# First Toeplitz blocks of a separable convolution: from the taps in SBUF instead of by way of DRAM

## The chip, the cores and the metric

The kernel runs on one core of a Trainium2 chip. The core has five engines with instruction queues of their own: PE (TensorE, matrix products), DVE (VectorE), ACT (ScalarE), POOL (GpSimd) and SP (SyncE, which here only issues transfers). Sixteen DMA engines move data between DRAM and the on-chip memory SBUF, whose 128 partitions are the rows of every tile. PE writes its results to PSUM. The metric is the device time of one execution in microseconds (us); lower is better. Everything is float32.

## The reference

The input x has 4 images of 64 channels of 256 x 256. Two layers are computed.

The first is a long convolution per channel. Its filter is the outer product of two 1-D filters of 256 taps for each channel, an "X" and a "Y" filter. Each comes from a small network with sine activations over a positional embedding, times an exponential decay:

```python
h = jnp.sin(freq * (z @ w1 + b1))
h = jnp.sin(freq * (h @ w2 + b2))
h = jnp.sin(freq * (h @ w3 + b3))
h = h @ wo
decay = jnp.exp(-t * jnp.abs(deltas))
return h * decay
...
k = jnp.einsum('ijk,imk->ijmk', hx, hy)[0]
...
y = jnp.fft.irfft2(u_f * k_f, s=(fft_size, fft_size))[..., :L, :L]
out = y + x * bias[:, None, None]
```

The FFTs are twice as long as the image, so this is a causal 2-D convolution, and since the filter is an outer product it splits into two 1-D passes. The second layer whitens the channels: a mean and a 64 x 64 covariance over every ninth pixel, five Newton-Schulz steps towards its inverse square root, and a product of that matrix with the centred pixels.

## The kernel before

**Taps.** The two filter networks run side by side as one 128-row problem (rows 0 to 63 the X filters, 64 to 127 the Y filters), at L154 to L176. Each layer is a matrix product, an argument reduction on DVE and a sine on ACT. The last step, L176, multiplies by the decay on DVE and writes `taps`, a part of the SBUF tile `scratch`: 128 rows of 256 taps, followed by 128 zeros. Row f * 64 + c holds the taps of filter f (0 or 1) of channel c, reversed in time.

**Toeplitz blocks.** A 1-D causal convolution by matrix products needs, for each filter and channel, the taps shifted by one from row to row. `load_toeplitz` (L188) makes them while loading: row p of a block is the row of taps read from element p on. A block tile `toep` holds, for a round of 8 channels (`CG`), 128 rows, 2 filters, 8 channels and 256 columns. It is loaded in halves of 64 rows (`half`); where the filter number and the half differ, the first 64 columns aren't needed and are skipped. The transfers read the taps from DRAM. For that the taps are stored at L177 (SP) and L178 (ACT) into a small array `g0_d`, which holds the 16 rows of the first round, and at L179 (POOL) into `g_d`, which holds all 128 rows and is read by the later rounds.

**The first round's loads.** L562 lists seven pairs of loads in order, as (filter, first channel, last channel): (0, 0, 2), (0, 2, 4), (0, 4, 6), (1, 0, 2), (0, 6, 8), (1, 2, 4), (1, 4, 8). The lower half of each pair is issued on SP, the upper on ACT. They wait for the stores into `g0_d`. Behind them SP issues the loads of the second image (L566) and, later, those of further images.

**Filler products.** `busy(n)` (L149) gives PE n products of an idle tile. PE takes its instructions in program order, so `busy(22)` at L181 stands between the last product of the filter networks and the first one of the convolution. Each float32 product is two instructions.

**Convolution.** The work goes over `steps`, pairs of a round g of 8 channels and an image n, and in each over channel pairs. The first pass (filter 0) is followed by a copy out of PSUM that swaps the halves (tile `o1`), the second pass (filter 1) by a multiply-add with the bias back into the x tile. In the steady state `group` (L394) does the first pass of one channel pair and the second pass of an earlier one together, in `toeplitz_products` (L203, products at L220). The first two channel pairs have no partner, so `half_group` (L266) does their first pass alone, in `toeplitz_alone` (products at L252, tile `ph`; copies at L286 on ACT and DVE). Its first products read both halves of the blocks of filter 0 of channels 0 and 1. The results go to the DRAM arrays `y_d`, and the ninth pixels are packed for the covariance.

**Whitening and output.** After the last convolution, the covariance (L333) and the Newton-Schulz steps follow, and then the output stage: tiles `yi` are loaded back from `y_d`, multiplied by the whitening matrix (L635), shifted (L639 ACT, L640 DVE) and stored to `out`.

**Order.** From L557 on everything stands under `manual_schedule`: every engine's instructions keep the order in which the program writes them. Each engine takes its own queue in order, and an instruction that waits holds what is behind it on that engine. Semaphores for the data dependences are put in by the framework.

Of the kernel before, what the change touches and what calls it, by code (L numbers as in the profile page):

```python
# [45 lines left out]
NB, C, L = 4, 64, 256  # L46
P, H2 = 128, 2
EMB, ORDER = 33, 64
PIX = L * L
CG = 8  # L50
HP = P // 2
# [13 lines left out]
def conv_whiten_kernel(ctx: ExitStack, tc: tile.TileContext, a: dict, out: bass.AP):  # L65
    nc = tc.nc
# [12 lines left out]
    g_d = dram.tile([P, GW], F32, tag="g", name="g_d")  # L79
# [17 lines left out]
    mask = const.tile([P, NB, H2, STEP], I32, tag="mask", name="mask")  # L97
    bias = const.tile([P, C], F32, tag="bias", name="bias")

    def load_x(t, g, n, c):  # L100
        nc.sync.dma_start(
            out=t[:, c : c + 2],
            in_=x[n, g][:, c : c + 2],
        )
# [16 lines left out]
    for n in range(NB):  # L121
        t = spool.tile([P, FP], F32, tag="samp", name=f"samp{n}")
# [7 lines left out]
    rows = const.tile([P, STEP], F32, tag="rows", name="rows")  # L130
# [8 lines left out]
    taps = scratch[:, 11:13, :].rearrange("p a w -> p (a w)")[:, 0:GW]  # L139
# [9 lines left out]
    def busy(times):  # L149
        p = psA.tile([P, P], F32, tag="psA", name="busy")  # L150
        for _ in range(times):
            nc.tensor.matmul(p, lhsT=idle[:, 0:P], rhs=idle[:, P : 2 * P], start=True, stop=True)  # L152

    hs, wt = [zw[:, u * P : (u + 1) * P] for u in range(2)], zw[:, L : L + P]  # L154
    for i in range(3):
        for u in range(2):
            pm = psA.tile([P, P], F32, tag="psA", name=f"pm{i}_{u}")
            nc.tensor.matmul(pm, lhsT=wt, rhs=hs[u], start=True, stop=True)  # L158
            half = slice(u * P, (u + 1) * P)
# [12 lines left out]
    for u in range(2):  # L172
        half = slice(u * P, (u + 1) * P)
# [2 lines left out]
        nc.vector.tensor_tensor(taps[:, half], pf, decay[:, half], ALU.mult)  # L176
    nc.sync.dma_start(out=g0_d[0:CG], in_=taps[0:CG])  # L177
    nc.scalar.dma_start(out=g0_d[CG:], in_=taps[ORDER : ORDER + CG])  # L178
    nc.gpsimd.dma_start(out=g_d, in_=taps)  # L179
    nc.gpsimd.tensor_copy(rows, mask[:, NB - 1, 0, :])  # L180
    busy(22)  # L181

    def new_toeplitz(g):


        return tpool.tile([P, 2, CG, L], F32, tag="toep", name=f"toep_{g}")

    def load_toeplitz(t, g, f, half, lo=0, hi=CG, issue=nc.sync):  # L188
        source, row = (g0_d, f * CG + lo) if g == 0 else (g_d, f * C + g * CG + lo)


        skip = 0 if f == half else HP
        issue.dma_start(
            out=t[half * HP : (half + 1) * HP, f, lo:hi, skip:],
            in_=bass.AP(
                tensor=source.tensor,
                offset=source.offset + row * GW + skip,
                ap=[[1, HP], [GW, hi - lo], [1, L - skip]],
            ),
        )  # L200


    def toeplitz_products(units, ks):  # L203
# [62 lines left out]
    def half_group(item, which):  # L266

        g, n, c, xt, o1s = item
        jobs = []
        for u in range(2):  # L270
            banks = [
                psA.tile([P, L], F32, tag="psA", name=f"ph{which}_{g}_{n}_{c + u}_{m}")
                for m in range(H2)
            ]
            jobs.append((banks, (o1s[u] if which else xt[:, c + u]), toep[g][:, which, c + u, :]))
        toeplitz_alone(jobs, which)
        if which == 0:
            for u in range(2):
                o1s.append(o1pool.tile([P, H2, L], F32, tag="o1", name=f"o1_{g}_{n}_{c + u}"))
        for m in range(H2):  # L280
            for u in range(2):
                ps = jobs[u][0][m]
                if which == 0:
                    copy = nc.vector.tensor_copy if u else nc.scalar.copy
                    for to, fr in ((slice(0, HP), slice(HP, P)), (slice(HP, P), slice(0, HP))):
                        copy(o1s[u][to, m], ps[fr])  # L286
                else:
                    ch = g * CG + c + u
                    nc.vector.scalar_tensor_tensor(
                        xt[:, c + u, m], xt[:, c + u, m], bias[:, ch : ch + 1], ps,  # L290
                        ALU.mult, ALU.add,
                    )
# [34 lines left out]
    def covariance(n):  # L327

        pc = psA.tile([P, C + 1], F32, tag="psA", name=f"pc{n}")
        for b in range(H2):  # L330
            for j in range(NJ):
                half = slice(C * (j % 2), C * (j % 2 + 1))
                nc.tensor.matmul(  # L333
                    pc[half],
                    lhsT=samp[n][:, b, j, 0:C],
                    rhs=samp[n][:, b, j, :],
                    start=(b == 0 and j < 2),
                    stop=(b == H2 - 1 and j >= NJ - 2),
                    skip_group_check=True,
                )  # L340
        nc.vector.scalar_tensor_tensor(cov, pc, 1.0 / NSAMP, cov, ALU.mult, ALU.add)
# [18 lines left out]
    def load_next():  # L360
        loaded[len(loaded)] = load_y(len(loaded))
# [32 lines left out]
    def group(first, second):  # L394

        units = []
        g1, n1, c1, x1, o1s1 = first
        g2, n2, c2, x2, o1s2 = second
        for u in range(2):
            job2 = (bank(f"p2_{g2}_{n2}_{c2 + u}"), o1s2[u], toep[g2][:, 1, c2 + u, :])  # L400
            job1 = (bank(f"p1_{g1}_{n1}_{c1 + u}"), x1[:, c1 + u], toep[g1][:, 0, c1 + u, :])
            units.append((job1, job2))

        toeplitz_products(units, orders[0])
        orders.reverse()
        for u in range(2):
            o1 = o1pool.tile([P, H2, L], F32, tag="o1", name=f"o1_{g1}_{n1}_{c1 + u}")
            for to, fr in ((slice(0, HP), slice(HP, P)), (slice(HP, P), slice(0, HP))):
                nc.scalar.copy(o1[to], units[u][0][0][fr])  # L409
            o1s1.append(o1)  # L410
            ch = g2 * CG + c2 + u
            nc.vector.scalar_tensor_tensor(  # L412
                x2[:, c2 + u], x2[:, c2 + u], bias[:, ch : ch + 1], units[u][1][0],
                ALU.mult, ALU.add,
            )

        store(second)
        pack(2.92)
# [138 lines left out]
    with tc.manual_schedule(  # L557
        engines={engines.PE, engines.SP, engines.DVE, engines.Activation, engines.Pool}
    ):
        toep = {0: new_toeplitz(0)}  # L560

        for f, lo, hi in ((0, 0, 2), (0, 2, 4), (0, 4, 6), (1, 0, 2), (0, 6, 8), (1, 2, 4), (1, 4, 8)):  # L562
            for half in range(2):
                load_toeplitz(toep[0], 0, f, half, lo, hi, nc.scalar if half else nc.sync)
        for c in range(0, CG, 2):
            load_x(x_tiles[1], *steps[1], c)  # L566
        for i, (g, n) in enumerate(steps):
            xt = x_tiles[i % 4]
            for c in range(0, CG, 2):
                item = (g, n, c, xt, [])  # L570
                if g == C // CG - 1 and n > 0 and c == 2:
                    covariance(n - 1)
                if len(pending) == 2:
                    group(item, pending.pop(0))
                else:
                    half_group(item, 0)
                pending.append(item)
                if i == 0 and c == 6:

                    fold = const.tile([P, C], F32, tag="fold", name="fold")  # L580
                    nc.vector.tensor_tensor(fold, ident[:, 0:C], ident[:, C:P], ALU.add)

                    nc.scalar.activation(bf[:, 0:1], samp[0][:, 0, 0, C : C + 1], AF.Sqrt)
                if i == 1 and c < CG - 2:
                    load_pick(c // 2 * 3, c // 2 * 3 + 3)

                if i + 2 < len(steps):
                    load_x(x_tiles[(i + 2) % 4], *steps[i + 2], c)
                if (i, c) in blocks:
                    tg, part = blocks[i, c]  # L590
                    if part == 0:
                        toep[tg] = new_toeplitz(tg)
                    lo = part % 2 * CG // 2
                    load_toeplitz(toep[tg], tg, part // 4, part // 2 % 2, lo, lo + CG // 2)
                for _ in range(early.get((i, c), 0)):
                    load_next()
        g, n, c, yt, _ = pending[0]
        for item in pending:
            half_group(item, 1)
            pack(1.0)  # L600
            store(item)

        pack()
        i15 = place(2 * C, rows=C).rearrange("p (u c) -> p u c", u=2)
        for u in range(2):
            nc.gpsimd.tensor_scalar(i15[:, u], ident[0:C, 0:C], 1.5, None, ALU.mult)  # L606
        ones = place(P, rows=C)
        nc.gpsimd.memset(ones, 1.0)
        for lo in range(CG // 2, CG, 2):
            pack_by_pe(g, n, yt, slice(lo, lo + 2))  # L610
        spin(4)
        covariance(NB - 1)
        while len(loaded) < len(homes):
            load_next()
        W, shift = whitening(i15, ones)
# [3 lines left out]
    for i, (n, q) in enumerate(pieces):  # L619
# [6 lines left out]
        for w in range(FP // 1024):  # L626
# [15 lines left out]
            if end % part == 0:  # L642

                issue = nc.sync if i == 0 or i + len(homes) >= len(pieces) else nc.gpsimd
# [61 lines left out]
```

## Time and profile before

| what | us |
|---|---|
| median of 3 runs (lowest, highest) | 903.08 (902.95, 903.26) |
| profiled execution: time | 903.93 |
| profiled execution: span from first to last instruction | 902.1 |
| PE busy (share of the span) | 781.2 (87%) |
| DVE busy | 581.5 (64%) |
| ACT busy | 395.5 (44%) |
| L220, the convolution's products: busy for each of the two passes | 579.5 |
| L252, the first round's lone products: start | 16.49 |
| whitening matrix starts from the finished covariance | 632 |

The page's busy figures are shares of the whole span. Up to about 613 us PE works through the convolution; from 670 us on the DMA engines are the busy ones, with 430 GB/s in most slices. The stretch around the change is the first 30 us. Times in the views count from the span's start. A row of the timeline gives the start, the length, the engine, the line, the operation, the tiles (output <- input), how many instructions were merged, and in brackets how long the engine had been idle before and what ended that. "SPq" and "ACTq" are the instruction queues that issue transfers; the length of such a row is the time taken to issue, not to move. A row of the chain of work names the instruction or transfer that the end was waiting for at that time. All three DRAM arrays of taps and blocks go by `g_d` in the profile's tile names.

### The profile page before, as it was taken

What the parts mean: (1) busy time and instruction counts of PE and PEld (TensorE: products, weight loads), DVE (VectorE), ACT (ScalarE), POOL (GpSimd) and SP (SyncE); (2) the same over time, 40 slices, a digit from 0 to 9 for tenths busy, and PEclk for the clock granted to TensorE, in tenths of its full rate; (3) what the DMA queues carried; (4) which work ended last, traced back from release to release, by engine and by line L of the source; (5) the groups of instructions that cost most, each with busy time, mean ns of one, the idle gap of its engine ahead of it and who ended that gap; (6) DMA issues with size and microseconds to landing.
All of it is one profiled execution on the core that took longest, in us unless ns stands there. A gap on an engine that the chain in (4) does not pass through costs nothing.

```text
span 902.1 us, 28046 instructions
## 1 busy us (share of the span) xinstructions
PE 781.2 (87%) x11928; PEld 647.5 (72%) x11928; DVE 581.5 (64%) x801; ACT 395.5 (44%) x676; POOL 14.5 (2%) x40
## 2 busy tenths in 40 slices
PE   8999999999999999999999999999999565666200
PEld 7999999999999999999999999999533111212000
DVE  3487778877888778877888877877688332233200
ACT  2655554545455555545454444442487232233200
POOL 1000000000000000000000000000010000000000
PEclk9999999999999999999999999999999766866755
DMA  7988889798788888888997899979999999999998
GB/s 209 327 262 252 242 261 271 234 273 251 247 263 261 244 264 259 258 250 267 293 275 241 285 351 356 335 237 390 375 401 429 430 432 432 429 434 430 430 430 355
DMA packets 117912, 285.61 MB, mean 317 GB/s; under 512 B 8891, under 2 KB 91116, under 8 KB 110108
## 3 DMA queue, kind: packets, MB, share of 16 engines
q1 hardware_dynamic: 113436, 244.94, 79.0%
q0 software_dynamic: 3056, 37.95, 10.0%
q8 instruction: 95, 1.56, 0.7%
q10 hardware_dynamic: 1296, 0.93, 0.4%
q14 instruction: 29, 0.24, 0.1%
HBM read 149.35 MB, written 134.44 MB: 315 GB/s over the span
## 4 chain that ended last, share of the span: by engine, by line
PE 74%; DMA 11%; another core or an unknown queue 7%; DVE 0%; issue 0%; SPq 0%; ACT 0%; POOLq 0%; DVEq 0%
PE p L220 64%; DMA out_dram<-yi 5%; DMA yi<-y_d 5%; PE po L635 4%; PE pc L333 2%; PE ph L252 1%; PE pk L300 1%; PE spin L442 1%; DMA toep<-g_d 0%; PE busy L152 0%; PE pm L158 0%; SPq L357 0%; DMA scratch<-in_zw_dram 0%; DVE yi L640 0%
## 5 line engine op out<-in xcount | busy, mean ns | idle before, releaser
L220 PE MATMUL p<-toep,x 64*64 64x64 f32 (+3 forms) x5040 | 579.5, 284 | 0.8 <-issue 0.8
L220 PE MATMUL p<-toep,o 64*64 64x64 f32 (+3 forms) x5040 | 579.5, 284 | 0.0
L220 PEld LDWEIGHTS p<-toep,x 64*128 64x128 f32 (+1 forms) x5040 | 535.7, 166 | 24.4 <-issue 1.3
L220 PEld LDWEIGHTS p<-toep,o 64*128 64x128 f32 (+1 forms) x5040 | 536.7, 166 | 10.7 <-issue 0.2
L409 ACT COPY o<-p 64x512 f32<-64x512 f32 x504 | 292.8, 581 | 294.2 <-PE p L220 286.6
L319 DVE COPY_PREDICATED samp<-mask,x 128x464 f32<-128x464 int32 (+3 forms) x351 | 297.2, 847 | 9.8 <-DVE x L412 0.2
L412 DVE SCALAR_TENSOR_TENSOR x<-x,bias,p 128x512 f32<-128x512 f32 x252 | 179.8, 744 | 121.3 <-PE p L220 117.3
L635 PE MATMUL po<-yi,chain 64*64 64x512 f32 x1024 | 143.7, 720 | 60.4 <-DMA yi<-y_d 60.4
L640 DVE TENSOR_SCALAR yi<-po,shift 128x512 f32<-128x512 f32 x128 | 96.1, 751 | 109.0 <-PE po L635 100.7
L635 PEld LDWEIGHTS po<-yi,chain 64*64 64x64 f32 x1024 | 48.0, 162 | 155.2 <-issue 150.5
L639 ACT ACTIVATE yi<-po,shift 128x512 f32<-128x512 f32 x128 | 88.0, 687 | 116.7 <-PE po L635 116.0
L333 PE MATMUL pc<-samp 128*64 128x65 f32 x464 | 14.9, 223 | 0.0
L333 PEld LDWEIGHTS pc<-samp 128*64 128x64 f32 x464 | 14.3, 137 | 0.3
L645 POOL DMA_DIRECT2D out_dram<-yi x19 | 10.5, 554 | 130.5 <-DMA out_dram<-yi 55.1
L606 POOL TENSOR_SCALAR chain<-ident 64x64 f32<-64x64 f32 x2 | 1.0, 519 | 606.6 <-PE ph L252 606.6
L286 DVE COPY o<-ph 64x256 f32<-64x256 f32 x8 | 3.4, 422 | 9.7 <-PE ph L252 9.6
L152 PE MATMUL busy<-idle 128*128 128x128 f32 x64 | 9.4, 307 | 0.0
L152 PEld LDWEIGHTS busy<-idle 128*128 128x128 f32 x64 | 8.9, 222 | 0.2 <-issue 0.2
L300 PE MATMUL pk<-x,pick 128*128 128x56 f32 (+1 forms) x72 | 8.3, 292 | 0.0
L300 PEld LDWEIGHTS pk<-x,pick 128*128 128x128 f32 x72 | 8.1, 192 | 0.1
L442 PE MATMUL spin<-ident 128*128 128x128 f32 x50 | 7.9, 292 | 0.0
L286 ACT COPY o<-ph 64x256 f32<-64x256 f32 x8 | 2.9, 368 | 10.7 <-DMA toep<-g_d 9.2
(93 smaller groups left out, 77.4 us busy)
## 6 DMA issues: line engine op xcount, KB each, us to landing
x<-in_x_dram SPq DMA_DIRECT2D x128, 512.0 KB, 5.3
y_d<-x SPq DMA_DIRECT2D x256, 256.0 KB, 3.5
yi<-y_d SPq DMA_DIRECT2D x32, 2048.0 KB, 15.6
out_dram<-yi POOLq DMA_DIRECT2D x17, 2048.0 KB, 67.7
out_dram<-yi SPq DMA_DIRECT2D x11, 2048.0 KB, 32.9
toep<-g_d SPq DMA_DIRECT2D x28, 256.0 KB, 6.3
toep<-g_d SPq DMA_DIRECT2D x29, 192.0 KB, 5.7
out_dram<-yi SPq DMA_DIRECT2D x4, 1024.0 KB, 32.8
```

The costliest lines, as they stand in the source:

```text
L152: nc.tensor.matmul(p, lhsT=idle[:, 0:P], rhs=idle[:, P : 2 * P], start=True, stop=True)
L220: mm = nc.tensor.matmul(ps[q : q + w, m, HP * k : L], lhsT=src[parts, k // 2, m * P + q : m * P + q + w], rhs=t[parts, : stop : -1] if k e ...
L300: nc.tensor.matmul(pk[:, b, :, 0:nj], lhsT=pick[:, (s - b) % STEP, :], rhs=yt[:, cs, b, s : s + STEP * (nj - 1) + 1 : STEP], start=(s == 0 ...
L319: nc.vector.copy_predicated(dst, m, src)
L333: nc.tensor.matmul(pc[half], lhsT=samp[n][:, b, j, 0:C], rhs=samp[n][:, b, j, :], start=(b == 0 and j < 2), stop=(b == H2 - 1 and j >= NJ ...
L409: nc.scalar.copy(o1[to], units[u][0][0][fr])
L412: nc.vector.scalar_tensor_tensor(x2[:, c2 + u], x2[:, c2 + u], bias[:, ch : ch + 1], units[u][1][0], ALU.mult, ALU.add,)
L442: nc.tensor.matmul(p, lhsT=ident, rhs=ident, start=True, stop=True)
L635: nc.tensor.matmul(po[u][halves[k]], lhsT=W[halves[u]], rhs=v[halves[u], k, cols], start=True, stop=True,)
L639: nc.scalar.activation(v[:, 0, cols], po[0], AF.Identity, bias=shift)
L640: nc.vector.tensor_scalar(v[:, 1, cols], po[1], shift, None, ALU.add)
L645: issue.dma_start(out=o[:, :, end - part : end], in_=v[:, :, end - part : end])
```

## The change

The blocks of filter 0 of channels 0 and 1 of the first round are no longer loaded from `g0_d`. A new function, `first_toeplitz`, loads them straight from `taps` in SBUF, one channel and one half a load: the source is one row of taps (one partition), read 64 times with a shift of one element. The halves go to SP and ACT as the loads did before. They stand directly behind the two stores into `g0_d`; the store into `g_d` on POOL and the fillers follow them in the text. The other six pairs of loads are unchanged.

```diff
     nc.sync.dma_start(out=g0_d[0:CG], in_=taps[0:CG])
     nc.scalar.dma_start(out=g0_d[CG:], in_=taps[ORDER : ORDER + CG])
-    nc.gpsimd.dma_start(out=g_d, in_=taps)
-    nc.gpsimd.tensor_copy(rows, mask[:, NB - 1, 0, :])
-    busy(22)
-
...
+    def first_toeplitz(t, f, half, c, issue):
+
+        skip = 0 if f == half else HP
+        row = f * ORDER + c
+        src = taps[row : row + 1, skip:L]
+        issue.dma_start(
+            out=t[half * HP : (half + 1) * HP, f, c, skip:],
+            in_=bass.AP(
+                tensor=src.tensor, offset=src.offset, ap=[list(src.ap[0]), [1, HP], [1, L - skip]]
+            ),
+        )
...
+    toep = {0: new_toeplitz(0)}
+    for c in range(2):
+        for half in range(2):
+            first_toeplitz(toep[0], 0, half, c, nc.scalar if half else nc.sync)
+    nc.gpsimd.dma_start(out=g_d, in_=taps)
+    nc.gpsimd.tensor_copy(rows, mask[:, NB - 1, 0, :])
+    busy(22)
...
-        toep = {0: new_toeplitz(0)}
-
-        for f, lo, hi in ((0, 0, 2), (0, 2, 4), (0, 4, 6), (1, 0, 2), (0, 6, 8), (1, 2, 4), (1, 4, 8)):
+
+        for f, lo, hi in ((0, 2, 4), (0, 4, 6), (1, 0, 2), (0, 6, 8), (1, 2, 4), (1, 4, 8)):
             for half in range(2):
                 load_toeplitz(toep[0], 0, f, half, lo, hi, nc.scalar if half else nc.sync)
```

## The prediction

> **What bounds the kernel now.** I read the page first, then the chain of work in order of time, then the first 30 us engine by engine, and last the transfers of that stretch. The page: PE leads, and the chain that ended last is PE for 74%, most of it the convolution at L220.
>
> ```profile
> PE 781.2 (87%) x11928; PEld 647.5 (72%) x11928; DVE 581.5 (64%) x801; ACT 395.5 (44%) x676; POOL 14.5 (2%) x40
> PE 74%; DMA 11%; another core or an unknown queue 7%; DVE 0%; issue 0%; SPq 0%; ACT 0%; POOLq 0%; DVEq 0%
> ```
>
> The chain in order of time (start, length, what) around the change:
>
> ```profile
> 10.68 0.30 DVE scratch L176
> ...
> 11.05 1.39 DMA g_d<-scratch
> 12.44 0.02 issue
> 12.46 3.90 DMA toep<-g_d
> 16.35 0.14 issue
> 16.49 6.02 PE ph L252 x58
> 22.51 60.85 PE p L220 x1072
> ```
>
> The taps are ready at 10.98. They go to DRAM (1.39 us), come back as Toeplitz blocks (3.90 us), and PE starts its first products at 16.49. From there the chain is PE without a break longer than 0.5 us until the whitening matrix at 632, and then the output stage. So a shift of the first product moves everything behind it, and the end, one for one. But the 5.3 us of transfers aren't what the change can save, as the timeline shows:
>
> ```profile
> 10.48 5.08 PE L152 MATMUL busy<-idle 128*128 128x128 f32 x44
> 12.46 6.59 SPq L193 DMA_DIRECT2D toep<-g_d  x7
> 12.46 5.82 ACTq L193 DMA_DIRECT2D toep<-g_d  x7
> 16.49 6.02 PE L252 MATMUL ph<-toep,x 64*128 64x256 f32 x64 [0.93 <-DMA toep<-g_d]
> 19.28 1.52 ACT L286 COPY o<-ph 64x256 f32<-64x256 f32 x4 [9.18 <-DMA toep<-g_d]
> ```
>
> The 22 filler products stand ahead of the first real one in PE's order and end at 10.48 + 5.08 = 15.56. PE idles for 0.93 us only. That is all that earlier blocks can give.
>
> **The change part by part.** *Removed:* two loads of two channels each (128 KB on SP, 96 KB on ACT), out of the chain's 1.39 + 3.90 us. *Added:* four loads of one channel, 64 KB each on SP, 48 KB each on ACT: 64 rows of 1024 bytes, or of 768, and 2 x (65,536 + 49,152) = 229,376 bytes, as many as before. What is new is the source: all 128 rows of a channel come out of one SBUF partition, partition 0 or 1.
>
> *Issue.* The small stores at L177 and L178 stay and go first: SP is free at 11.05 + 0.29 = 11.34, ACT at 11.05 + 0.54 = 11.59. The new loads wait for the same DVE result as those stores, so they issue at about 11.4 and 12.0 on SP, 11.6 and 12.2 on ACT (0.6 us each, the median issue at L193). First packets: the store issued at 11.05 moved its first about 11.81 (0.76 us later), the old loads issued at 12.46 about 13.95 (1.5 us). So 12.1 to 12.9; I take 12.5.
>
> *Moving.* The trace of before shows no read out of one or two partitions; I bound it by three rows of the DMA view (the stores of 11.6 to 12.2 us, the old loads of 14 to 16 us, and a stretch of the output stage):
>
> ```profile
> DMA packets 37, 0.03 MB, mean 43 GB/s; under 512 B 21, under 2 KB 37, under 8 KB 37
> ...
> DMA packets 483, 0.38 MB, mean 190 GB/s; under 512 B 48, under 2 KB 483, under 8 KB 483
> ...
> DMA packets 760, 11.14 MB, mean 429 GB/s; under 512 B 80, under 2 KB 80, under 8 KB 80
> ```
>
> Fast end: the old loads' 190 GB/s, 229 KB in 1.2 us, landed at 13.7, hidden by the fillers. Slow end: the two stores read 24.6 KB out of 16 partitions in the 0.31 us from 11.81, 4.9 GB/s a partition, the fastest that the trace shows out of few; two partitions give 9.9 GB/s, 23.2 us, landed at 35.7. Between them lies the third row: 429 GB/s over 16 engines is 27 GB/s for one. I take that, as an estimate: sixteen engines that queue at one place in SBUF get about what one engine moves. The stores' burst was too short to be a limit, and the old loads read DRAM, so neither end is near. 229,376 bytes at 27 GB/s are 8.5 us: landed at 21.0, first product at 21.1 with the chain's 0.14 us. Against 16.49 that is +4.6 us.
>
> [...]
>
> *The clock.* PE would idle from 15.56 to 21.1, 5.5 us. What that does is seen in the output stage, timeline first, then the busy time in stretches of 2 us (the seventh entry from the left, after POOL, is the granted clock):
>
> ```profile
> 700.41 1.93 PE L635 MATMUL po<-yi,chain 64*64 64x512 f32 x16
> 708.39 5.36 PE L635 MATMUL po<-yi,chain 64*64 64x512 f32 x32 [6.06 <-DMA yi<-y_d]
> ```
>
> ```profile
> 702.00:704.00 2.00, 0.34 (x4) 0.00 (x0) 1.06 (x2) 0.89 (x2) 0.53 (x1) 1.00 0.96 410
> 704.00:706.00 2.00, 0.00 (x0) 0.00 (x0) 0.00 (x0) 0.00 (x0) 0.00 (x0) 0.76 1.03 442
> 706.00:708.00 2.00, 0.00 (x0) 0.00 (x0) 0.00 (x0) 0.00 (x0) 0.00 (x0) 0.50 1.07 459
> ```
>
> After 6.06 us of idleness the clock was at 0.50, and 32 products took 5.36 us where twice 1.93 = 3.86 was the pace before: 1.5 us lost. The same in the first round: +1.5 us. It falls about 2.7 us into the idle stretch, so the bounds are 0 (blocks in by 18.2) and 1.7 (half of the 3.4 us for which the clock stays down after 708.39).
>
> *Moved at no cost, and what covers it.* The store at L179 is alone on POOL before and after; none of the new loads is on POOL, so it still issues at 11.59, and SP first needs it at 29.86. SP and ACT each issue one DMA more (8 for 7), 0.6 us, beside PE. The other twelve block loads stand behind the new ones in the same two queues, and SP's waits show that a load can be held until an earlier one has landed (three times, 1.9 us in all). Channels 2 and 3 (224 KB) follow at the 258 GB/s that 16 to 18 us showed: 0.9 us after 21.0, needed 3 us after the first product. The blocks (1, 0, 2) may be held until the first new load lands; with the 5 us to landing of such loads they are in at 26, needed at 21.1 + 6.0 + 1.5 = 28.6. ACT's copies at L286 queue behind its own issues: three or four of 0.6 us after 21.0 end by 23.4, and the first copy is due at 24.1. If one of these covers is gone, it costs a microsecond or so, inside the range. The x loads that SP issued from 19.09 go out about 25 and land 8.2 us later, at 33; the first group on that image runs at 31.3 before and 37.4 after.
>
> *Sum.* +4.6 + 1.5 = +6.1 us. The profiled execution took 903.93 us (span 902.1 and 1.8 around it), 0.85 above the median of 903.08; the shift is taken over to the median: 909.2 us.
>
> **The rivals.** *Not slower: the source is no brake.* The bytes are the same, and a round trip of 1.39 us goes. Above 60 GB/s the blocks are in by 16.35 (229 KB in 3.85 us), above 75 GB/s they hide behind the fillers wholly: -0.93 us, 902.2. For it: the old loads too read 64 overlapping rows of the same 1.5 KB, and ran at 190 GB/s. Against it: all of that is DRAM.
>
> *One engine each.* The new loads' source has one partition where the stores had eight; if each queue is served by a single engine, the change spreads less than it says. Two engines at 27 GB/s, one for each queue, take 131 KB / 27 = 4.9 us: landed at 17.4, first product at 17.5, +1.0 us, 904.1. On the same engine it is the forecast again. Nothing in the trace decides it; a DMA share far under 0.9 would show it.
>
> *Slower still.* Under 20 GB/s the move takes over 11.5 us: above 912.2, up to 23.2 us, first product at 35.8, +19.3 + 1.5, 923.9. For it: the stores' row. Against it: their 16 packets on ACT's queue needed only 6.2% of the engines' time.
>
> **How the numbers follow.** Forecast (20 to 41 GB/s): 55%; its own range is 904.8 (41 GB/s: landed at 18.1, +1.7 and no clock loss) to 912.2. No brake: 24%. Between, 41 to 60 GB/s or two engines: 6%. Slower still: 13%. A gain over 0.2% (1.8 us, about what a measurement of this kernel can tell from no change): 2%, since only 0.93 us of idleness is there to be had. So slower 0.68, same 0.30, faster 0.02. No brake can't be left out of the range, so it reaches down to 902.0; upward to 913.0, which leaves some 12% above and 2% below.
>
> **What would show it.** Right: the wait ahead of L252 grows from 0.93 to about 5.5 us; the DMA rows of 13 to 21 us show about 27 GB/s with the engines nearly all busy; the clock is 0.50 around 20 us; the rest of the chain is the old one, later. Wrong: the first product directly behind the fillers at 15.6 (no brake); a fast read but a wait ahead of the second half group, of the first L220 product or of ACT's copies (a cover gone); a low DMA share (one engine each). The step most likely to be mis-sized is the 27 GB/s.

## The result and the profile after

The changed kernel takes 910.84 us (median of 4 runs, 910.67 to 910.86), the one before 903.02 us (902.48 to 903.26). The ratio is 1.0087 with a 95% interval of 1.0075 to 1.0100: 7.8 us slower. The profiled execution took 910.86 us, with a span of 909.1 against 902.1.

The chain of waits of the changed kernel, in order of time (start, length, what):

```profile
12.29 10.17 DMA toep<-scratch
22.60 7.54 PE ph L268 x54
30.14 490.74 PE p L236 x8543
```

The step through DRAM is gone from the chain, and one load out of SBUF that lands 10.17 us after its issue stands in its place; through DRAM it had been 1.39 + 3.90. The timeline of the same stretch shows what PE does in it (in brackets the idle time before a row and what ended it):

```profile
10.53 5.08 PE L152 MATMUL busy<-idle 128*128 128x128 f32 x44
11.44 1.22 SPq L189 DMA_DIRECT2D toep<-scratch  x2
11.68 1.45 ACTq L189 DMA_DIRECT2D toep<-scratch  x2
16.33 0.67 PE L268 MATMUL ph<-toep,x 64*128 64x256 f32 x2 [0.72 <-DMA toep<-scratch]
22.60 7.54 PE L268 MATMUL ph<-toep,x 64*128 64x192 f32 x62 [5.60 <-DMA toep<-scratch]
26.79 1.51 ACT L302 COPY o<-ph 64x256 f32<-64x256 f32 x4 [16.63 <-PE ph L268]
```

SP's first block, issued at 11.44, landed 4.8 us later, at 16.24. The first two of the 64 lone instructions (one product) need only that block and can start. The next one needs the upper half of channel 1, which is ACT's second load; so the other 62 wait until 22.60. The issues and landings of 11 to 14 us (how many, KB each, median us to landing) show who else is held up:

```profile
g_d<-scratch POOLq DMA_DIRECT2D x1, 192.0 KB, 10.2
toep<-scratch SPq DMA_DIRECT2D x2, 64.0 KB, 7.5
...
toep<-scratch ACTq DMA_DIRECT2D x2, 48.0 KB, 10.3
```

Even the store into `g_d` (2.3 us before) now takes 10.2 us, and nobody needs it yet. It wasn't slow as a whole: 47 of its 64 packets moved between 14 and 16 us, and a few of the rest came as late as 21 us. The busy times in stretches of 2 us (behind POOL: granted clock, share of the DMA engines' time, GB/s):

```profile
16.00:18.00 2.00, 0.67 (x2) 0.29 (x2) 0.00 (x0) 0.00 (x0) 0.00 (x0) 1.00 0.87 39
18.00:20.00 2.00, 0.00 (x0) 0.00 (x0) 0.00 (x0) 0.00 (x0) 0.00 (x0) 0.89 0.70 23
20.00:22.00 2.00, 0.00 (x0) 0.00 (x0) 0.00 (x0) 0.00 (x0) 0.00 (x0) 0.50 0.75 114
22.00:24.00 2.00, 1.40 (x7) 1.43 (x9) 0.00 (x0) 0.00 (x0) 0.00 (x0) 0.50 0.68 157
...
26.00:28.00 2.00, 2.00 (x23) 1.92 (x24) 1.04 (x3) 1.17 (x4) 0.00 (x0) 0.91 1.07 269
```

Between 18 and 20 us the DMA engines are occupied for 70% of their time and move 23 GB/s; in the kernel before they moved 190 GB/s at 94% between 14 and 16 us. The clock falls to 0.50 at about 19.6 and is back at about 26.4 (worked out from the means of the two stretches, 0.89 and 0.91), so 62 products take 7.54 us where 64 took 6.02.

Behind that the profiles run alongside each other. The first product at L236 (L220 before) comes 7.6 us later (29.89 against 22.26), the last lone products of the convolution 6.7 (620.29 against 613.60), and the span is 7.0 us longer.

### The profile page after: what moved, and what is told of

It reads as the page before. It is cut to its first block, busy times and chain, and to the rows that moved or that the text cites. A ratio compares the mean times of both kernels' runs of the same rounds, so it can differ in the third digit from the quotient of the medians.

```text
span 909.1 us, 28051 instructions
## 1 busy us (share of the span) xinstructions
PE 782.4 (86%) x11928; PEld 648.3 (71%) x11928; DVE 581.2 (64%) x801; ACT 394.8 (43%) x676; POOL 14.5 (2%) x40
## 4 chain that ended last, share of the span: by engine, by line
PE 73%; another core or an unknown queue 11%; DMA 8%; SPq 0%; DVE 0%; issue 0%; ACTq 0%; POOLq 0%; DVEq 0%
PE p L236 64%; DMA out_dram<-yi 5%; PE po L650 4%; PE pc L349 2%; DMA yi<-y_d 2%; PE ph L268 1%; DMA toep<-scratch 1%; PE pk L316 1%; PE spin L458 1%; PE busy L152 0%; SPq L373 0%; PE pm L158 0%; DMA scratch<-in_zw_dram 0%; DVE yi L655 0%
## 5 line engine op out<-in xcount | busy, mean ns | idle before, releaser
L236 PE MATMUL p<-toep,x 64*64 64x64 f32 (+3 forms) x5040 | 578.5, 284 | 0.5 <-issue 0.5
L236 PE MATMUL p<-toep,o 64*64 64x64 f32 (+3 forms) x5040 | 578.7, 284 | 0.0
L236 PEld LDWEIGHTS p<-toep,x 64*128 64x128 f32 (+1 forms) x5040 | 534.9, 166 | 24.1 <-issue 0.7
L236 PEld LDWEIGHTS p<-toep,o 64*128 64x128 f32 (+1 forms) x5040 | 535.9, 166 | 11.2 <-issue 0.3
L302 DVE COPY o<-ph 64x256 f32<-64x256 f32 x8 | 3.4, 422 | 17.3 <-PE ph L268 17.2
L268 PE MATMUL ph<-toep,x 64*128 64x192 f32 (+3 forms) x64 | 8.2, 396 | 6.3 <-DMA toep<-scratch 6.3
L660 POOL DMA_DIRECT2D out_dram<-yi x19 | 10.5, 552 | 130.3 <-DMA out_dram<-yi 58.1
L268 PEld LDWEIGHTS ph<-toep,x 64*128 64x128 f32 x64 | 7.5, 232 | 7.0 <-issue 6.9
L302 ACT COPY o<-ph 64x256 f32<-64x256 f32 x8 | 2.9, 366 | 18.3 <-PE ph L268 18.1
## 6 DMA issues: line engine op xcount, KB each, us to landing
yi<-y_d SPq DMA_DIRECT2D x32, 2048.0 KB, 18.3
```

Source lines behind the costliest of these rows:

```text
L236: mm = nc.tensor.matmul(ps[q : q + w, m, HP * k : L], lhsT=src[parts, k // 2, m * P + q : m * P + q + w], rhs=t[parts, : stop : -1] if k e ...
L268: mm = nc.tensor.matmul(ps[m][:, HP * k : L], lhsT=src[parts, k // 2, m * P : (m + 1) * P], rhs=t[parts, : stop : -1] if k else t[parts, : ...
L660: issue.dma_start(out=o[:, :, end - part : end], in_=v[:, :, end - part : end])
```

## The experiments

Single executions begin their fillers between 9.8 and 10.5 us, so I compare the time from the start of the 44 filler instructions to the point from which the lone products run on (the third instruction of the 64, or the first where there is no second wait). It is 6.01 us before and 12.07 after. "Time" is device time, beside it the kernel before on the same chip in the same series. The four runs with other rows, `rows_0_4_crossed`, `many_parts` and `no_shift` were each timed once; in the others the time is a median.

| run | fillers to products, us | lone products, us | time, us | before, us |
|---|---|---|---|---|
| before | 6.01 | 6.02 (64) | 903.02 | |
| after | 12.07 | 7.54 (62) | 910.84 | 903.02 |
| rows_0_0 | 12.14 | 8.14 (62) | 910.04 | 902.75 |
| rows_0_32 | 12.10 | 8.43 (62) | 913.44 | 902.75 |
| rows_0_4 | 9.61 | 7.75 (62) | 907.54 | 902.75 |
| rows_0_64 | 9.85 | 7.29 (62) | 907.47 | 902.75 |
| rows_0_4_crossed | 7.28 | 7.58 (62) | 905.99 | 902.22 |
| many_parts | 5.00 | 6.05 (64) | 901.44 | 903.01 |
| no_shift | 11.83 | 7.33 (62) | 909.45 | 903.01 |
| dram_single | 6.43 | 5.83 (62) | 902.38 | 903.01 |
| one_channel | 8.13 | 8.62 (62) | 906.58 | 902.42 |
| one_half | 6.14 | 6.03 (64) | 902.61 | 902.42 |
| fillers | 11.48 | 6.45 (64) | 911.42 | 903.01 |
| wide_fillers | 12.12 | 5.83 (62) | 908.53 | 902.22 |

### Which partitions share an outlet

Four runs change only the rows that the new loads read. In the diffs the row numbers are all that differs.

```diff
-        row = f * ORDER + c
+        row = 0            # rows_0_0
+        row = 32 * c       # rows_0_32
+        row = 4 * c        # rows_0_4
+        row = 64 * c       # rows_0_64
```

> The changed kernel, but both channels read row 0 of the taps, so channel 1 of the first round is convolved with channel 0's filter (this part of the computation is changed). Theory 'one place' (partitions 0 and 1 share one outlet that all sixteen engines queue at, about 24 GB/s): nothing changes, first product at 22.6 us, time 910.8. Rival 'one partition' (each partition is an outlet of its own, 12 GB/s apiece): the same bytes out of half the outlets take 19 us instead of 9.6, first product at about 32, time 920.

> The changed kernel, but channel 1 reads row 32 of the taps (another channel's filter: this part of the computation is changed). [...] Rival 'neighbours share' (partitions next to each other share an outlet, far ones don't): half the time in the queue, last block in at 12.85 + 4.8 = 17.7, first product at 17.8, time 904.3. Rival 'one partition': 22.6, 910.8.

> The changed kernel, but channel 1 reads row 4 of the taps (another channel's filter: this part of the computation is changed). [...] Rival 'one partition': nothing changes, 22.6 and 910.8. Rival 'any read out of SBUF is that slow' (engines, not the outlet): 22.6 and 910.8.

> The changed kernel, but channel 1 reads row 64 of the taps, a filter of the second pass (this part of the computation is changed). [...] Rivals 'one partition' and 'any read out of SBUF is that slow': 22.6 and 910.8.

The rows of the timeline on which the comparison rests, for rows 0 and 32 and for rows 0 and 4:

```profile
10.44 5.08 PE L152 MATMUL busy<-idle 128*128 128x128 f32 x44
22.54 8.43 PE L268 MATMUL ph<-toep,x 64*128 64x192 f32 x62 [5.76 <-DMA toep<-scratch]
...
9.94 5.08 PE L152 MATMUL busy<-idle 128*128 128x128 f32 x44
19.55 7.75 PE L268 MATMUL ph<-toep,x 64*128 64x192 f32 x62 [3.20 <-DMA toep<-scratch]
```

Rows 0 and 0 behave as rows 0 and 1 do (12.14 and 12.07 us): one partition feeds the sixteen engines as fast as two neighbours. So the limit isn't one of the single partition. Rows 0 and 32 are the same again (12.10), so "neighbours share" falls too. Rows 0 and 4, and rows 0 and 64, are faster (9.61 and 9.85), so the limit isn't one of any read out of SBUF either. Of the rows tried, 0, 1 and 32 thus share a limit, and 4 and 64 stand outside it. What is shared, called an outlet here, stands in no view, and how the other rows group isn't shown. The time of rows_0_32, 913.44 us from one run, is higher than its first product explains; its profile has 1.2 us of pauses in PE's issue and 0.5 of waiting for POOL's queue where that of the changed kernel has 0.5 of pauses, its lone products take 0.9 us more (by estimate the clock was low for about 10 us instead of 6.8), and the rest I can't place.

But at the changed kernel's pace two outlets would have halved the time of the reads (115 KB each at 24 GB/s, last block in at 12.85 + 4.8 = 17.7 us, first product at 17.8, 7.3 from the fillers' start), and they didn't. Both queues hold row 0 in front and the other row behind, so one more run let ACT issue channel 1 first:

```diff
-            first_toeplitz(toep[0], 0, half, c, nc.scalar if half else nc.sync)
+            first_toeplitz(toep[0], 0, half, 1 - c if half else c, nc.scalar if half else nc.sync)
```

> As the run with rows 0 and 4 (channel 1 has another channel's filter: this part of the computation is changed), but ACT issues channel 1 first, SP channel 0 first. With rows 0 and 4 the last block came at 19.4 and not at 17.7. Theory: the two outlets were used one after the other, because both queues held row 0 in front; crossed, each outlet is busy from the start: last block in at 17.7 to 18.3, first product at 17.8 to 18.5, time 904.3 to 905. Rival (reads out of few partitions have a common limit of about 33 GB/s, wherever they lie): 19.5 to 20.3, time 907.5.

The products start 7.28 us after the fillers, as the theory had it, but the landings show that this is partly for another reason. The crossing also puts ACT's load of channel 1, for which the third instruction waits, first in its queue: it landed at 17.4 us, while SP's second load came at 18.2 and ACT's second at 18.5. From the first packet to the last landing the four loads took 6.1 us (38 GB/s), against 7.3 us (31 GB/s) for rows 0 and 4 in the old order and 9.8 us in the changed kernel; two outlets at the changed kernel's pace would take 4.9. So the order of the loads counts, by 1.2 of the 2.3 us, and the rival's 33 GB/s was passed. That both outlets were busy from the start is not shown: in both runs the packets of these loads up to 12.9 us are all of SP's queue, from 12.1 us with rows 0 and 4 and from 12.4 in the crossed run. The time, 905.99, is above the 904.3 to 905 expected, because the clock fell after all. The timeline of this run:

```profile
15.77 0.67 PE L268 MATMUL ph<-toep,x 64*128 64x256 f32 x2 [0.46 <-DMA toep<-scratch]
17.52 7.58 PE L268 MATMUL ph<-toep,x 64*128 64x192 f32 x62 [1.08 <-DMA toep<-scratch]
```

and its busy times:

```profile
16.00:18.00 2.00, 0.92 (x7) 0.55 (x7) 0.00 (x0) 0.00 (x0) 0.00 (x0) 0.97 0.62 121
18.00:20.00 2.00, 2.00 (x12) 1.71 (x9) 0.00 (x0) 0.00 (x0) 0.00 (x0) 0.50 0.80 159
20.00:22.00 2.00, 2.00 (x20) 1.95 (x19) 0.08 (x1) 0.00 (x0) 0.00 (x0) 0.67 1.06 269
```

PE stood still for 0.46 and 1.08 us only, and the clock was low from about 17.9 to 21.3 all the same.

### Is it SBUF, the shift, or the size of the loads?

`many_parts` reads 64 partitions, one row each. `no_shift` reads the same row 64 times from its beginning. `dram_single` leaves the source in DRAM and splits the first pair of loads by channel.

```diff
 # many_parts
-            in_=bass.AP(
-                tensor=src.tensor, offset=src.offset, ap=[list(src.ap[0]), [1, HP], [1, L - skip]]
-            ),
+            in_=taps[f * ORDER : f * ORDER + HP, skip:L],
 # no_shift
-    ap=[list(src.ap[0]), [1, HP], [1, L - skip]]
+    ap=[list(src.ap[0]), [0, HP], [1, L - skip]]
 # dram_single, on the kernel before
-        for f, lo, hi in ((0, 0, 2), (0, 2, 4), ...
+        for f, lo, hi in ((0, 0, 1), (0, 1, 2), (0, 2, 4), ...
```

> The changed kernel, but the four new loads read 64 partitions of the taps, one row each without a shift, so the blocks of channels 0 and 1 are no Toeplitz blocks (this part of the computation is changed). Same bytes, same issues, same destination. Theory 'one place': with the source spread there is no queue, the blocks are in before the fillers end, first product at 15.6, time 902.1 to 902.3. Rival 'any read out of SBUF is that slow': 22.6 and 910.8.

> The changed kernel, but all 64 rows of a block are the same unshifted row of taps, so every read starts at the row's beginning, aligned (this part of the computation is changed). If the reads that start in the middle of a line cost the difference between the 24 GB/s measured and the 27 GB/s forecast, the last block is in at 12.85 + 8.5 = 21.4, first product at 21.5, time 909.5. If not, 22.6 and 910.8. If the shift were the whole trouble (overlapping reads), the blocks would be in before the fillers end: 15.6 and 902.1.

> The kernel before, with the first pair of loads split into one channel a load, still from DRAM. Theory: each queue issues one load more, 0.6 us, and the last of the four blocks is in up to 0.6 us later: first product at 16.5 to 17.1, time 903.0 to 903.7. Rival 'one channel a load is the trouble' (small loads, more waits): several us more.

With 64 partitions as the source, the timeline has no wait ahead of the lone products:

```profile
10.33 5.08 PE L152 MATMUL busy<-idle 128*128 128x128 f32 x44
15.33 6.05 PE L266 MATMUL ph<-toep,x 64*128 64x256 f32 x64
```

and the new loads land 2.4 (SP) and 2.9 us (ACT) after their issue in the median, in place of 7.5 and 10.3:

```profile
toep<-scratch SPq DMA_DIRECT2D x2, 64.0 KB, 2.4
toep<-scratch ACTq DMA_DIRECT2D x2, 48.0 KB, 2.9
```

Same bytes, same issues, same destination: with the narrow source the whole wait is gone, so the source is its cause. This run takes away the shift together with the narrow source; `no_shift` tells the two apart. Its 901.44 us is one run, 1.6 below the median of before, where 0.93 of idleness had gone; the single run doesn't carry the rest. Without the shift the wait ends 0.24 us earlier (11.83 against 12.07, one execution each), so the shift is at most a small part. `dram_single` has a ratio of 0.9995 (0.9985 to 1.0005) to before: one load more in each queue costs nothing that can be measured in the time, and "one channel a load" isn't the trouble.

### Half the bytes, a quarter of the bytes

```diff
 # one_channel: only channel 0 from SBUF
-    for c in range(2):
+    for c in range(1):
...
+        for f, lo, hi in ((0, 1, 2), (0, 2, 4), ...
 # one_half: only the upper half of channel 0 from SBUF
-    for c in range(2):
-        for half in range(2):
-            first_toeplitz(toep[0], 0, half, c, nc.scalar if half else nc.sync)
+    first_toeplitz(toep[0], 0, 1, 0, nc.scalar)
...
+        load_toeplitz(toep[0], 0, 0, 0, 0, 2, nc.sync)
+        load_toeplitz(toep[0], 0, 0, 1, 1, 2, nc.scalar)
```

> The changed kernel with channel 0 alone from SBUF and channel 1 from DRAM. Theory 'one place': 115 KB at 24 GB/s, 4.8 us, last SBUF block in at 17.7, the DRAM blocks behind them in the same queues about then or up to 1 us later: first product at 17.8 to 18.7, time 904.3 to 905.3. If the queue's cost were a fixed wait and not one by the byte: 22.6 and 910.8.

> The kernel before, with one of the four blocks, 48 KB (upper half of channel 0), from SBUF and the other three from DRAM. The SBUF block has 49 KB at 24 GB/s, 2.0 us from 12.85, in at 14.9, before the DRAM blocks. Theory: the read out of one partition keeps all engines occupied while the DRAM blocks start at 13.95, so what is saved in bytes (176 KB for 224) is lost in waiting: first product between 16.0 and 17.0, time 902.6 to 903.6. Rival (the two run beside each other): 15.6 to 16.0, time 902.1 to 902.5, faster than both kernels.

With one channel the wait ends at 18.30, 8.13 us after the fillers' start; expected was 17.8 to 18.7. What ended it is a DRAM block behind the SBUF block in ACT's queue. The SBUF blocks themselves were in at 17.8, 5.5 us after their first packet, where twice the bytes took 9.8. So the cost goes roughly by the byte; the fixed wait of the rival is ruled out. The time is 1.0044 times that of before (1.0030 to 1.0058), or 4.2 us more, where the expected 904.3 to 905.3 meant 1.3 to 2.3: the lone products took 8.62 us, against 5.83 at a clock of 1.00 (`wide_fillers`) and 7.58 in the crossed run, so by estimate the clock fell here too. With one half block the ratio is 1.0005 (0.9996 to 1.0014): no difference, and the products start 6.14 us after the fillers, against 6.01. The SBUF block lands 4.0 us after its issue and the DRAM blocks about as long after theirs as before. So neither of the two shares tried gains.

### The clock

```diff
 # fillers
-    busy(22)
+    busy(51)
 # wide_fillers: the same 22, each 300 columns wide
+        width = 300 if times == 22 else P
+        p = psA.tile([P, width], F32, tag="psA", name="busy")
...
-            nc.tensor.matmul(p, lhsT=idle[:, 0:P], rhs=idle[:, P : 2 * P], start=True, stop=True)
+            nc.tensor.matmul(p, lhsT=idle[:, 0:P], rhs=idle[:, P : P + width], start=True, stop=True)
```

> The changed kernel with 51 filler products for 22: PE is busy until 22.3 instead of 15.6, so nothing but the idle stretch is taken away. Theory: the first product stays at 22.6, the clock stays up, the 62 lone products take 6.0 us instead of 7.5 and the time falls by 1.5 to 1.7 us to about 909.2. Rival (the clock costs nothing at the end, since later work has slack): 910.8.

> The changed kernel with the last 22 filler products 300 columns wide for 128. In the run with 51 fillers the first product came at 21.99, the clock stayed at 1.00 and the convolution was 2.5 us ahead at 518 us, but PE then stood still for 2.25 us in a stretch that the chain calls issue. This run keeps PE's number of instructions. Theory: the fillers end about 22, the clock stays up, the lone products take 6.0 to 6.4 us, the pauses are those of the changed kernel, and the time is 909.0 to 909.5. Rival (what is won at the clock is taken back later, whatever the instructions): 910.8 with a pause or a wait of over 1 us between 30 and 630 us.

With 51 fillers the clock stayed at 1.00, and the chain was 2.5 us ahead of the changed kernel's at the covariance (518.42 against 520.88). Then it lost that again:

```profile
518.42 3.64 PE pc L349 x116
522.06 0.26 PE p L236 x4
522.33 2.25 issue
524.58 36.77 PE p L236 x633
```

PE waited for 2.25 us for nothing that the profile shows. The time, 911.42 (ratio 1.0096, 1.0080 to 1.0113), missed the expectation. The wide fillers keep the number of PE's instructions; the pause in that place is then the 0.45 us of the changed kernel, and the timeline is

```profile
10.40 11.28 PE L153 MATMUL busy<-idle 128*128 128x300 f32 x44
21.61 0.70 PE L269 MATMUL ph<-toep,x 64*128 64x256 f32 x2
22.52 5.83 PE L269 MATMUL ph<-toep,x 64*128 64x192 f32 x62 [0.22 <-DMA toep<-scratch]
```

The 62 products take 5.83 us and not 7.54, and the time is 6.3 us above before (908.53 against 902.22; ratio 1.0070, 1.0057 to 1.0084) where the change alone was 7.8 above. That agrees with the 1.5 us of the clock, but the two intervals overlap, so the times alone don't show it; the 1.7 us in the profile is the firmer reading. That the long pause in `fillers` comes from its 58 more instructions is a guess; the runs show only that it wasn't there without them.

## Why the prediction was right, and where its sizes were off

The forecast was 909.2 us, slower, with a range of 902.0 to 913.0; measured were 910.84. Its two terms, the wait for the blocks and the lost clock, are the two that the runs found. The wait was forecast as +4.6 us and came out as +6.1 (22.60 against 16.49); the products behind it were forecast as +1.5 and came out as +1.5 (7.54 for 62 instructions against 6.02 for 64).

- *What there was to gain.* The idle 0.93 us ahead of the first product is about what `many_parts` wins at the products (5.00 us from the fillers' start in place of 6.01).
- *First packets, 12.5.* The first packet of the new loads was at 12.68, 1.24 us after its issue, between the old loads' row (1.5 us) and the stores' (0.76). The forecast was 0.18 us too early.
- *Moving, 27 GB/s, 8.5 us.* From 12.68 to the last landing at 22.46 the 229 KB took 9.8 us, 23 GB/s (the expectations of the runs reckon with 12.85 and 24 GB/s, which moves them by less than 0.2 us). This is the term that was most off, by 1.3 us. At first the pace was the forecast one: from 12.85 to 14.3 us, when only SP's queue moved packets, it was 28 GB/s.

```profile
DMA packets 39, 0.04 MB, mean 28 GB/s; under 512 B 0, under 2 KB 39, under 8 KB 39
```

  From 18 to 19 us it was 21 GB/s. The shift accounts for at most 0.24 us (`no_shift`). The store into `g_d` (192 KB) fell into the same stretch; what it cost the loads wasn't tested, and the rest stays open.
- *The choice of the row.* That sixteen engines which queue at one place get what one engine moves was an estimate; the row experiments show that two rows can be as slow as one (12.07, 12.10 and 12.14 us) and another pair faster (9.61 and 9.85), and the one-channel run that the cost goes roughly by the byte (5.5 us for half the bytes, 9.8 for all). Why its pace is about that of one engine is not shown.
- *The clock, +1.5.* The low clock cost 1.7 us (7.54 against 5.83 us for 62 products). That the size fitted so well is partly luck: with the same wait `no_shift` lost 1.5 us, `rows_0_0` 2.3 and `rows_0_32` 2.6 (7.33, 8.14 and 8.43 against 5.83). What was wrong is the lower bound: no loss had been expected with the blocks in by 18.2, and in the crossed run the clock fell although the products ran on from 17.52.
- *Covers.* They held. ACT's copies at L302 waited for PE, not for ACT's own issues; the first products at L236 follow without a wait; the x loads of the second image went out at 26.52 (25 had been estimated). ACT's issues ended at 24.93 and not at 23.4, still 1.9 us ahead of its first copy.
- *The sum.* +6.1 us was forecast; at L236's first product the shift was 7.6, and the spans differ by 7.0, so it was handed on to the end one for one to within 0.9 us. The median moved by 7.8, since the profiled execution before lay 0.9 us above the median (903.93 and 903.02), and the one after lies on it (910.86 and 910.84).

Of the rivals, "the source is no brake" is refuted by the 23 to 39 GB/s of 16 to 20 us. "One engine each" is refuted by the engines' share of 0.70 to 0.87 in that stretch: two of sixteen would be 0.13. "Slower still" would have needed under 20 GB/s.

## What to carry to other kernels

Before a transfer is taken out of a chain, ask how wide its new source is: 229 KB out of two neighbouring partitions took 9.8 us here from the first packet to the last landing (and out of a single one as long), out of 64 partitions about 2.6, and the way through DRAM took 5.3 with the issues and the store included. Look at what the waiting engine does meanwhile, too: fillers covered all but 0.93 us of the old round trip, so the best case was 0.1% and the bad one, with the clock lost on top, nearly 0.9%. If narrow sources can't be avoided, the choice of the rows counts (0 and 4 were read in 7.3 us, 0 and 1 in 9.8), and the load for which the waiting engine waits first should stand first in its queue (in the crossed run ACT's first load was in at 17.4 us, its second at 18.5).

## What the runs showed that was not expected

- *Two issues behind the slow transfers took about 7 us each.* In the changed kernel one issue on SP lasted 7.19 us and one on ACT 6.75, with medians of 0.6 (duration in ns: least, median, greatest):

```profile
L201 SPq DMA_DIRECT2D toep<-g_d x10: 573/592/7187, 12.8 to 55.9; - x10
L201 ACTq DMA_DIRECT2D toep<-g_d x6: 581/604/6747, 13.2 to 24.3; - x6
```

  In the kernel before, the longest issues of such loads were 1.80 us on SP and 0.66 on ACT; what exactly held the two isn't shown. ACT had no work of its own between 10.16 and 26.79 us, so whether that would have waited too isn't shown either.
- *The length of the low clock doesn't follow that of the wait.* Worked out from the means of the 2 us stretches, the low clock lasted 3.4 us in the crossed run and with rows 0 and 64, where the longest waits were 1.08 and 3.36 us, and 6.8 us in the changed kernel and with rows 0 and 4, where they were 5.60 and 3.20. With rows 0 and 0 and rows 0 and 32 it had set in at 17.1 and 18.3 us and was still 0.50 at 24; by estimate it lasted about 10 us (their lone products lost 2.3 and 2.6 us, where those of the changed kernel lost 1.7 in 3.8 us of low clock). It set in between 2.2 and 4.6 us after the fillers had ended. One long wait wasn't needed: in the crossed run it fell after two gaps of 0.46 and 1.08 us inside 2.2 us. After a single gap of 0.93 us (before) it stayed at 1.00, and after single gaps of 0.73 us (`dram_single`) and 1.06 us (`one_half`) the lone products took 5.83 us (62) and 6.03 us (64), no longer than at a clock of 1.00. What sets the moment and the length isn't shown.
